# A graph network's layer pair: edge counts moved beside the keys, one addition moved forward, and one PSUM bank passed from the preparation to the groups' sums

## The chip, the cores and the metric

The kernel runs on one core of a Trainium2 chip. A core has TensorE (PE, matrix multiply; its weight loads are listed apart as PEld), VectorE (DVE), ScalarE (ACT), GpSimd (POOL) and queues for DMA, of which this kernel uses mainly SyncE's (SP). They run side by side and wait for one another by semaphores. SBUF is the memory that they work in; PSUM, eight banks of 128 x 512 float32, is where TensorE puts its results. The metric is device time in microseconds (us) of one execution.

## The reference

32 graphs ("batches") of 512 nodes with 128 features each, and a weight for each pair of nodes; about one weight in 16 is not zero. Cut to what matters:

```
# layer 0, for each batch
adj  = adj + I ; degree = adj.sum(2) ; dinv = degree ** -0.5
x    = layernorm(x + dinv * (adj @ (dinv * (x @ W0))) + b0)
# layer 1, for each batch, each pair of nodes i, j
pre  = (x_j @ W1[:128]) + (x_i @ W1[128:]) + b1          # 512 x 512 x 128
msg  = gelu(layernorm(pre) * g1 + be1)
agg  = sum over j of msg[i, j] * adj[i, j]
x    = layernorm(x + layernorm([x, agg] @ W2 + b2) * g2 + be2)
```

The degree of a node and the number of its edges (weights that are not zero) are both row sums, of the weights and of a mask. All of x, W and adj are float32.

## The kernel before, in words

**Groups.** The kernel works on edges only. The weights that aren't zero are sorted into "slots": in each block of 128 x 128 node pairs every row gives its t-th edge to slot t. A batch has 8 such slots of 4 groups, one slot of a single group (the node's own edge) and two slots of 4 groups for edges left over and gathered across rows: 41 groups a batch, called position 0 to 40 here, 1312 in all. A group takes four steps, each on its own engine, and one a turn later than the one before:

- `pairs` (lines 711 to 726, TensorE): 16 bf16 matmuls (lines 724 and 725) into one PSUM bank of the pool `ps_u`; from position 33 on 8 more instructions on float32 (line 720).
- `sums` (line 734, VectorE) adds a row of `ac` to that bank and writes `u_sb` in SBUF. That frees the bank. Positions 33 to 40 have no such step: there ScalarE reads the bank itself.
- `weights` (line 749, GpSimd) makes `sw`, `messages` (line 763, ScalarE) makes `m`, four activations.
- `aggregate` (line 772, TensorE) adds `m` times `sw` to the batch's sum `agg`, 8 instructions.

In the turn of group g the program issues pairs of g, aggregate of g-3, sums and weights of g-1, messages of g-2 (`pass_on`, lines 843 to 853).

**Preparation.** In the same turns other generators run in small steps (a step ends at each `yield`), and each has a stretch of turns in `plan` (lines 799 to 806): `layer0` of the next batch takes 26 steps in positions 0 to 21, `shared` of this batch 45 steps in positions 8 to 27, `lists`, `parts`, `factors` and `more` lie around the change of batch, and `finish` of the batch before goes step by step from position 2 on. Layer 0 transposes the weights (lines 249 and 261), sums the degrees (line 260), makes a mask of zeros (line 263), counts the edges by summing the mask (line 293, four ScalarE instructions for four blocks of rows), works out `dinv` on GpSimd (lines 277 to 287), adds x and b0 (line 289, GpSimd), scales (lines 297 and 302), multiplies (line 311), normalizes (lines 318 and 191 to 211) and makes the `key` by which edges are sorted (lines 357 to 366, four blocks of rows, one a step; lines 361 and 362 are VectorE's). The counts of edges are read by one line, 499 in `shared`, where they are compared with the edges listed.

**PSUM.** Eight banks: three for `pairs` (`ps_u`, line 80), one for `agg`, four for every result of the preparation (`ps`, line 82, through `bank`, line 213).

**Order.** Line 860 fixes the order of ScalarE, GpSimd and VectorE as the program issues it. The order of TensorE and of SyncE's queue is not written: a planner sets it when the program is built, by the program's order and by what it holds ready at a moment. The turns before the first group (line 838) lie outside line 860, and there the planner orders every engine.

## Time and profile before

| what | us |
|---|---|
| three runs: median (lowest, highest) | 4014.03 (4009.70, 4014.95) |
| the profiled execution, time | 4011.64 |
| its span on the core | 4009.9 |
| TensorE matmul busy in the span | 3766.3 (94%) |
| VectorE / ScalarE / GpSimd busy | 3263.9 / 2791.9 / 2225.5 |
| first matmul of the first group, from the span's start | 62.5 |

The profile is that of one execution. Busy time is the time in which an engine worked; a matmul's end is modelled, so that the share says little on how near TensorE is to its peak. A line of the waits names the engine and line that waited, what ended the wait, the total in us, how many times, and the longest one. A line of the timeline gives the start and the duration in us, engine, line, operation, tiles, shape and count, and in brackets the idle time before it with what ended it. Batch 16 serves as the example: its position 0 starts at 2023.3 us, its position 9 at 2046.7 and its position 14 at 2063.4.

### The profile page before, as it was taken

What the parts mean: (1) busy time and instruction counts of PE and PEld (TensorE: products, weight loads), DVE (VectorE), ACT (ScalarE), POOL (GpSimd) and SP (SyncE); (2) the same over time, 40 slices, a digit from 0 to 9 for tenths busy, and PEclk for the clock granted to TensorE, in tenths of its full rate; (3) what the DMA queues carried; (4) which work ended last, traced back from release to release, by engine and by line L of the source; (5) the groups of instructions that cost most, each with busy time, mean ns of one, the idle gap of its engine ahead of it and who ended that gap; (6) DMA issues with size and microseconds to landing.
All of it is one profiled execution on the core that took longest, in us unless ns stands there. A gap on an engine that the chain in (4) does not pass through costs nothing. (4 is left out here: it accounts for less than half of the span.)

```text
span 4009.9 us, 108439 instructions
## 1 busy us (share of the span) xinstructions
PE 3766.3 (94%) x39744; PEld 3510.3 (88%) x39744; DVE 3263.9 (81%) x10645; ACT 2791.9 (70%) x8321; POOL 2225.5 (55%) x2526
## 2 busy tenths in 40 slices
PE   5999999999999999999999999999999999999997
PEld 5988889888899888898888998888998889888887
DVE  6888888888887888888888888888888888788892
ACT  4777677676776766776767767667767677676664
POOL 4555565555655555655556555556555565555554
PEclk7999999999999999999999999999999999999998
DMA  3444444444444444444444444444444444444442
GB/s 85 107 109 106 114 101 106 107 107 105 113 102 106 108 106 110 106 106 106 107 105 113 102 106 108 106 112 104 106 105 108 105 108 106 108 107 105 98 105 56
DMA packets 902107, 419.99 MB, mean 105 GB/s; under 512 B 724304, under 2 KB 882192, under 8 KB 901568
## 3 DMA queue, kind: packets, MB, share of 16 engines
q1 hardware_dynamic: 901344, 412.52, 44.1%
q8 instruction: 317, 5.19, 0.5%
q14 instruction: 222, 1.82, 0.1%
q0 software_dynamic: 224, 0.46, 0.1%
HBM read 227.15 MB, written 13.76 MB: 60 GB/s over the span
## 5 line engine op out<-in xcount | busy, mean ns | idle before, releaser
L749 POOL TENSOR_TENSOR sw<-mt,a_t 128x512 f32<-128x512 bf16 x1056 | 1216.8, 1164 | 918.1 <-PE agg L772 764.0
L772 PE MATMUL agg<-sw,m 128*128 128x128 f32 x10496 | 1495.7, 285 | 76.2 <-POOL sw L749 46.1
L724 PE MATMUL u<-c,s 128*128 128x128 bf16 x15744 | 1433.9, 220 | 84.0 <-DVE u_sb L734 80.3
L763 ACT ACTIVATE m<-u_sb,r 128x128 f32<-128x128 f32 x4096 | 1294.0, 395 | 142.3 <-DVE u_sb L734 57.8
L772 PEld LDWEIGHTS agg<-sw,m 128*128 128x128 f32 x10496 | 1304.5, 192 | 94.2 <-POOL sw L749 51.3
L724 PEld LDWEIGHTS <-s 128*128 128x128 bf16 x15744 | 1191.2, 98 | 115.0 <-issue 40.9
L725 PE MATMUL u<-be,sd_rows 128*128 128x128 bf16 x5248 | 1148.6, 220 | 20.7 <-DMA sd_rows<-sd_ds 14.6
L734 DVE TENSOR_TENSOR u_sb<-u,ac 128x512 f32<-128x512 f32 x1056 | 713.4, 676 | 200.6 <-PE u L725 177.1
L725 PEld LDWEIGHTS <-sd_rows 128*128 128x128 bf16 x5248 | 512.7, 98 | 30.7 <-issue 20.0
L763 ACT ACTIVATE m<-u,r_s 128x128 f32<-128x128 f32 x1024 | 288.3, 363 | 251.6 <-PE agg L772 247.4
L533 ACT COPY sent<-pl 128x352 f32<-128x352 f32 x512 | 228.9, 447 | 315.9 <-PE pl L537 278.8
L687 DVE TENSOR_SCALAR s<-raw,node_p 128x2052 bf16<-128x2052 bf16 (+1 forms) x352 | 421.5, 1197 | 20.6 <-DMA raw<-idx_ds 11.9
L720 PE MATMUL u<-ac,sj 128*128 128x128 f32 x2048 | 437.8, 296 | 0.0
L749 POOL TENSOR_TENSOR sw<-mt,sent 128x512 f32<-128x512 bf16 x256 | 296.4, 1163 | 229.0 <-PE agg L772 176.2
L537 PEld LDWEIGHTS pl<-a_t,sj 128*128 128x128 f32 x2048 | 316.2, 191 | 60.7 <-issue 59.2
L457 DVE MAX8 a_t<-key 128x8 f32<-128x128 f32 x1024 | 301.2, 294 | 34.5
L537 PE MATMUL pl<-a_t,sj 128*128 128x176 f32 x2048 | 327.4, 313 | 1.3 <-POOL a_t L505 1.3
L522 DVE TENSOR_SCALAR sj<-pj,node_p 128x512 f32<-128x512 f32 x256 | 187.7, 745 | 153.8 <-PE pj L526 153.8
L720 PEld LDWEIGHTS u<-ac,sj 128*128 128x128 f32 x2048 | 310.0, 192 | 0.4
L458 DVE FIND_INDEX8 idx_m<-a_t,key 128x8 uint32<-128x128 f32 x1024 | 291.4, 285 | 0.0
L311 PEld LDWEIGHTS pconv<-s,a_t 128*128 128x128 f32 x1024 | 141.3, 214 | 57.1 <-ACT s L297 55.4
L361 DVE SCALAR_TENSOR_TENSOR key<-pv,a_sum,c_sum 128x512 f32<-128x512 f32 x128 | 95.7, 748 | 108.3 <-PE pv L365 108.3
(178 smaller groups left out, 4788.8 us busy)
## 6 DMA issues: line engine op xcount, KB each, us to landing
raw<-idx_d SPq DMA_DIRECT2D x256, 513.0 KB
raw<-idx_ds SPq DMA_DIRECT2D x64, 513.0 KB
a_nat<-in_adj_dram SPq DMA_DIRECT2D x32, 1024.0 KB
sd_rows<-sd_d SPq DMA_DIRECT2D x768, 12.0 KB
xs<-in_x_dram SPq DMA_DIRECT2D x32, 256.0 KB
out_dram<-o_sb SPq DMA_DIRECT2D x32, 256.0 KB
mt<-s SPq DMA_TRANSPOSE x352
raw<-idx_ds SPq DMA_DIRECT2D x32, 129.0 KB
```

The source lines that it names most:

```text
L457: nc.vector.max(found, k)
L458: nc.vector.max_index(idx[:, n, h : h + 8], found, k)
L533: nc.scalar.copy(sent[:, n - 1], pt[:, : SHARED * WIDE].rearrange("p (k w) -> p k w", w=WIDE))
L537: nc.tensor.matmul(pt[:, k * WIDE : (k + 1) * WIDE], sj[:, n, k * P : (k + 1) * P], at[:, n, :], start=True, stop=True,)
L687: nc.vector.tensor_scalar(s.rearrange("p (k e) -> p k e", k=3), raw, node_p, None, ALU.is_equal)
L720: nc.tensor.matmul(pu[:, c, :], place, state[b]["ac"][:, q, 0, :], start=first, stop=False)
L724: nc.tensor.matmul(pu[:, c, :], here, c3[:, k, c, :], start=(first and k == 0), stop=False)
L725: nc.tensor.matmul(pu[:, c, :], dev[:, q, c, :], be9, start=False, stop=(c == C - 1))
L734: nc.vector.tensor_tensor(u, pu, a if t == EXTRA else bcast(a[:, q, :], C), ALU.add)
L749: nc.gpsimd.tensor_tensor(sw, mt[:, 0] if t == EXTRA else mt[:, :, q, :], a, ALU.mult)
L763: nc.scalar.activation(m[:, c, :], u[:, c, :], AF.Gelu, scale=r[:, k : k + 1])
L772: nc.tensor.matmul(st["agg"][:, c, :], m[:, c, :], sw[:, c, :], start=(begin and c == 0), stop=(end and c == C - 1),)
```

## The change

Three edits. The four counts of edges leave the step of layer 0 that makes the scaled features (turn of position 6) and go one by one into the four steps that make the keys (positions 18 to 21), each in front of its two VectorE instructions; they read the same mask and write the same `edges`. The addition of x and b0 on GpSimd moves one step forward, ahead of the six small instructions on the degrees; the number of steps stays. `ps_u` gets four banks instead of three, and `ps` three instead of four. No instruction is added or taken away.

```diff
-    ps_u = ctx.enter_context(tc.tile_pool(name="ps_u", bufs=3, space=PSUM))
+    ps_u = ctx.enter_context(tc.tile_pool(name="ps_u", bufs=4, space=PSUM))
     ps_g = ctx.enter_context(tc.tile_pool(name="ps_g", bufs=1, space=PSUM))
-    ps = ctx.enter_context(tc.tile_pool(name="ps", bufs=4, space=PSUM))
+    ps = ctx.enter_context(tc.tile_pool(name="ps", bufs=3, space=PSUM))
...
-        yield from pause(2)
+        yield
+        xb = node.tile([P, C, D], F32, tag="t2", name=f"xb_{b}")
+        nc.gpsimd.tensor_tensor(xb, xs, bcast(rows["b0"], C), ALU.add)
+        yield
 
         deg1 = small.tile([P, C], F32, tag="deg1", name=f"deg1_{b}")
...
         nc.gpsimd.tensor_tensor(dinv2, dinv, dinv, ALU.mult)
-        xb = node.tile([P, C, D], F32, tag="t2", name=f"xb_{b}")
-        nc.gpsimd.tensor_tensor(xb, xs, bcast(rows["b0"], C), ALU.add)
-
-        for q in range(C):
-            copied = small.tile([P, N], BF16, tag="copied", name=f"counted_{b}_{q}", bufs=1)
-            nc.scalar.activation(copied, mask[:, q, :], AF.Copy, accum_out=edges[:, q : q + 1])
 
         s = node.tile([P, C, D], F32, tag="t1", name=f"s_{b}")
...
         for q in range(C + 1):
             if q:
+
+                copied = small.tile([P, N], BF16, tag="copied", name=f"counted_{b}_{q}", bufs=1)
+                nc.scalar.activation(copied, mask[:, q - 1, :], AF.Copy, accum_out=edges[:, q - 1 : q])
                 here = key[:, q - 1, :]
                 nc.vector.scalar_tensor_tensor(here, pt, a_sum[:, q - 1 : q], c_sum, ALU.add, ALU.add)
```

## The prediction

> **What bounds the kernel now.** I read the page's busy times first, then the waits, then the timeline of one batch, engine by engine.

> ```profile
> PE 3766.3 (94%) x39744; PEld 3510.3 (88%) x39744; DVE 3263.9 (81%) x10645; ACT 2791.9 (70%) x8321; POOL 2225.5 (55%) x2526
> ...
> PE u L724 <- DVE u_sb L734: 80.3, 69, 2.2
> PE agg L772 <- POOL sw L749: 46.1, 30, 1.6
> PE agg L772 <- ACT m L763: 30.0, 20, 1.5
> ```

> TensorE is the busiest, and its longest waits are those the bank edit aims at: pairs waiting until VectorE has emptied a bank of `ps_u`, 69 waits, two a batch. The next two answer them: aggregate waiting for GpSimd and ScalarE. The question is whether taking the first away saves time or lengthens the others. TensorE in batch 16, then VectorE, then GpSimd:

> ```profile
> 2044.19 0.33 PE L724 MATMUL u<-c,s 128*128 128x128 bf16 x3 [0.84 <-DVE u_sb L734]
> ...
> 2046.74 0.22 PE L724 MATMUL u<-c,s 128*128 128x128 bf16 x1 [1.50 <-DVE u_sb L734]
> ...
> 2065.97 1.16 PE L772 MATMUL agg<-sw,m 128*128 128x128 f32 x8 [1.55 <-POOL sw L749]
> ```

> ```profile
> 2032.42 0.69 DVE L641 TENSOR_TENSOR u<-pu,b_row 128x512 f32<-128x512 f32 x1 [2.05 <-PE pu L638]
> ...
> 2057.07 0.36 DVE L196 BATCH_NORM_AGGREGATE mv_l<-stats_l 128x2 f32<-128x6 f32 x4
> ```

> ```profile
> 2057.53 0.23 POOL L199 TENSOR_SCALAR ve_l<-mv_l 128x4 f32<-128x4 f32 x1 [3.39 <-DVE mv_l L196]
> ...
> 2064.75 2.29 POOL L749 TENSOR_TENSOR sw<-mt,a_t 128x512 f32<-128x512 bf16 x2
> ```

> ```profile
> 2032.40:2057.40 25.00, 22.66 (x250) 22.11 (x248) 24.30 (x91) 21.76 (x70) 17.85 (x21) 0.93 0.39 76
> 2057.40:2066.00 8.60, 7.05 (x89) 6.63 (x86) 8.57 (x26) 6.13 (x19) 7.64 (x16) 1.00 0.43 112
> 2066.00:2098.00 32.00, 31.99 (x270) 27.28 (x271) 18.09 (x27) 19.66 (x56) 11.34 (x10) 1.00 0.49 134
> ```

> Columns of the stretches: length, then busy us of PE, PEld, DVE, ACT, POOL. A chain shows. At 2032.42 VectorE gets the finish of the last batch from TensorE. From there it works 24.30 of 25.00 us without one wait, until the statistics of the next batch's layer 0. GpSimd, which had stood 3.39 us in front of them, works 7.64 of 8.60 us until the `sw` of group 11, and TensorE stands before that group's aggregate. From 2066 on TensorE never stops (31.99 of 32.00). Timed in batches 2 to 29 of the trace the pieces repeat: 22.87 (L641 to line 318) + 2.15 (to the last L196) + 0.40 + 8.07 (power of L187 to the end of `sw` 11) + 0.05 = 33.5 us, then 89.1 us of TensorE until the next L641, of which 88.6 is the least. So the waits at positions 8 and 9 lie inside a stretch that VectorE and GpSimd time: TensorE has 3.9 us to spare there (25.00 - 22.66, and 8.60 - 7.05), whatever it is spent on.

> [...]

> **The change part by part.** *Four banks for the sums.* Pairs 8 needs the bank of group 4 instead of 5, and 0.84 + 1.50 = 2.34 us a batch of waits go. TensorE then stands earlier at aggregate 10, which can't begin before `m` of group 10 (2061.07, behind the normalization on ScalarE), and at aggregate 11, whose `sw` ends at 2065.92 as before: nothing on VectorE or GpSimd in that chain moves. In an unchanged order the gain is nil. It is real only so far as work from behind aggregate 11 comes in front of it, and TensorE's order is the planner's. In the trace it keeps the program's order, except where something was late in its eyes (pairs 9 lies among the matmuls of line 311 and aggregate 5). With 2.3 us more in hand it will see aggregate 10 late, and it now has a bank to fill the gap: pairs 15 needs the sums of group 11 (2059.32 to 2060.00) instead of group 12 (2063.14 to 2063.82). It runs in the 1.5 us before aggregate 10, or in the gap before 11. One pairs is 16 matmuls, 0.055 us apart: 0.88 us. 31 batches have a next layer 0: 31 x 0.88 = 27.3 us. Ends: 0 (order kept) and 1.76 us a batch (pairs 16 too, its bank free at 2063.82), 54.6.

> *Counts on ScalarE.* Four times 0.75 us (starts 2043.20, 2043.93, 2044.69, 2045.44) leave the front of the scaled features. Those then wait for `dinv`, and `m` of group 5 comes 1.7 to 3 us sooner than 2048.07; aggregate 5 and line 311 follow. VectorE reads line 311's result at 2055.25 straight behind its own work, so this shortens nothing; it keeps TensorE from finding a new wait at aggregate 5. At the new place each count falls into ScalarE's waits for the shared lists (1.93 us, three a batch); the last has none, and delays the last copy of line 533 from 2097.72 to 2098.47, and VectorE's line 553, which needs that copy and now the count too (its output takes the mask's place), started at 2098.53. With the time of a semaphore I put 0.1 us a batch, as VectorE then works without a pause up to a short wait of TensorE at position 31: 3.1 us; ends 0 and 0.75 (23 us). Queued behind the last count are messages 20 and 21, whose aggregates come over 1.8 us after their old end.

> *x + b0.* 1.27 us of GpSimd move from behind the degrees to before `sw` 5, and `dinv` of batch 16's turn comes 1.27 us later, 2044.3: still before the old start of the scaling (2046.07). `sw` 5 has 9 us until its aggregate. Nothing, in the loop; without that cover it would cost 1.27 a batch.

> *Before the first group* both do help: the chain is serial there.

> ```profile
> 14.01 1.37 POOL L289 TENSOR_TENSOR xb<-xs,b_row 128x512 f32<-128x512 f32 x1
> ...
> 18.43 0.20 POOL L287 TENSOR_TENSOR dinv<-dinv 128x4 f32<-128x4 f32 x1
> ...
> 18.91 0.63 ACT L293 ACTIVATE counted<-mask 128x512 bf16<-128x512 bf16 x1
> 19.45 0.19 ACT L293 ACTIVATION_READ_ACCUMULATOR counted<-mask 128x1 f32 x1
> 19.54 1.12 ACT L297 ACTIVATE s<-psup,dinv 128x128 f32<-128x128 f32 x4
> ```

> `dinv` is there at 18.35 and the scaling starts at 19.54: 1.2 us, once (ends 0 and 2).

> *Three banks for the preparation.* I followed the banks through batch 16. Most are held at positions 14 to 20: a held chunk of the shared lists, a block of the keys, the chunk at work. At position 19 the third chunk (2088.69) finds the key's bank just free (2088.44), or else waits for the copy of the first (2088.73). The first transposes of layer 0 can't go ahead of the finish any more, but pairs 3 can fill that gap. I put 0; ends 0 and 0.65 us (one chunk without a second bank: copy 0.45 and 0.2 of waits) in each of four steps.

> Sum against the profiled 4011.6: - 27.3 + 3.1 - 1.2 = 3986.2. The median of the runs is 2.4 above the profiled one, so 3987 to 3989; I say 3987.

> **Rivals.** *The wait only moves*: TensorE's order stays, the 2.34 us reappear at aggregates 10 and 11. For it: the order departs from the program's in few places. 4014 + 3.1 - 1.2 = 4016. *Two groups come forward*: pairs 16 fits before aggregate 11 too, if the planner believes GpSimd as late as it is. 4014 - 54.6 + 2 = 3961. *Slower, the preparation starves*: at positions 18 to 21 a count of 0.75 us stands before the copy that holds a bank, beside the key's bank. If one chunk a step waits 0.4 us (between 0.05 and 0.65) in the stretch where TensorE has no slack: 4 x 0.4 x 31 = 50 us, 4014 - 26 + 50 = 4038. It decides from 0.22 us a step, where it eats the 0.88. Against it: the times above leave room of 0.15 us or more. The change does do what it says; only its worth hangs on the order.

> **How the numbers follow.** Forecast 0.50, two groups 0.15, moved wait 0.15, starved 0.20. Runs tell a change of about 0.2% (8 us) from none: faster 0.65, same 0.15, slower 0.20. The range runs from 3955, under the two groups' time, to 4026, which holds the moved wait and the mild part of the starved case; some 0.05 below and 0.13 above are left. The forecast's own range is 3975 to 4000.

> **What would show it.** Right: no pairs waiting for L734 at positions 8 and 9; on TensorE pairs 15 before aggregate 11; the wait of L772 for `sw` still there and GpSimd's 8.07 us unchanged; from aggregate 11 to the next L641 88.2 instead of 89.1; the first pairs at 61.3 instead of 62.5. Wrong: pairs 15 behind aggregate 11 (moved wait), TensorE waiting at L537, L526 or L365 for a copy or for L361 (starved), or a chain from L641 to `sw` 11 that isn't 33.5 any more.

## The result, and the profile after

The changed kernel takes 4019.82 us (median; 4016.50 to 4021.18), the kernel before on the same chip 4012.14 (4008.56 to 4018.11). The ratio is 1.0017, 95% interval 1.0009 to 1.0024: slower by 7 us, where 25 less was forecast. The span of the profiled execution is 4017.3 us, 7.4 more than before.

The page of the changed kernel, busy times (us, share of the span, instructions):

```profile
PE 3792.3 (94%) x39744; PEld 3525.4 (88%) x39744; DVE 3265.4 (81%) x10645; ACT 2783.8 (69%) x8321; POOL 2226.0 (55%) x2526
```

TensorE is busy 26.0 us longer with the same 39744 matmuls. Its waits in the changed kernel:

```profile
PE agg L772 <- ACT m L763: 68.0, 35, 2.1
PE agg L772 <- POOL un L645: 43.2, 30, 1.4
...
PE agg L772 <- POOL sw L749: 6.3, 7, 1.5
...
PE u L724 <- DVE u_sb L734: 3.0, 3, 2.0
```

What the fourth bank was to remove is gone: 80.3 us of pairs waiting for line 734 have become 3.0. In its place aggregates wait: 68.0 us for messages (30.0 before), and 43.2 in a new place, aggregate 5 in position 8. (GpSimd's line 645 is named because it happens to end then; ScalarE starts message 5 only at 2054.26, behind the scaled features, and the aggregate goes at 2054.86.) So the wait moved. TensorE also waits 31 times now for the scaled features at line 308 (20.7 us in all). TensorE in batch 16 of the changed kernel:

```profile
2069.50 1.48 PE L772 MATMUL agg<-sw,m 128*128 128x128 f32 x8 [2.11 <-ACT m L763]
...
2072.05 0.53 PE L724 MATMUL u<-c,s 128*128 128x128 bf16 x3
...
2073.86 1.16 PE L772 MATMUL agg<-sw,m 128*128 128x128 f32 x8
...
2075.28 0.33 PE L724 MATMUL u<-c,s 128*128 128x128 bf16 x3
```

The first line is aggregate 10, the third aggregate 11. Pairs 14 (from 2072.05) and pairs 15 (from 2075.28) lie behind them as before. The bank that pairs 15 needs was free from 2067.90 on, when the sums of group 11 ended on VectorE; it was not used. After the wait of 2.11 us, three matmuls take 0.53 us that take 0.33 later on: in the trace they start 0.107 us apart instead of 0.056. The stretches of this batch, cut as in the prediction (length, busy us of PE, PEld, DVE, ACT, POOL, then TensorE's granted clock):

```profile
2040.30:2065.30 25.00, 23.09 (x277) 22.65 (x275) 24.29 (x91) 19.00 (x62) 17.87 (x21) 1.00 0.37 85
2065.30:2073.90 8.60, 6.49 (x59) 5.83 (x56) 8.56 (x26) 6.14 (x19) 7.65 (x16) 0.80 0.35 89
2073.90:2105.90 32.00, 31.99 (x269) 27.09 (x269) 18.00 (x26) 21.26 (x60) 11.34 (x10) 1.00 0.55 133
```

VectorE works 24.29 of 25.00 (24.30 before), then GpSimd 7.65 of 8.60 (7.64): the chain in front of aggregate 11 is the old one. Over batches 2 to 29 its pieces are 22.86 + 2.15 + 0.40 + 8.07 + 0.05 us against 22.87 + 2.15 + 0.40 + 8.07 + 0.05. New in the second stretch is a granted clock of 0.80. Pairs 14 runs slowly and fills the gap in front of aggregate 11, so the waits for `sw` fall from 46.1 to 6.3 us although `sw` comes no sooner. Over the whole execution the mean granted clock is 0.979 instead of 0.985; 0.006 x 4017 us is 24 us, by my estimate most of the 26.0 us that TensorE is busy longer.

Where the 7.4 us of span came from, from the starts in both traces: aggregate 11 to the next line 641 takes 89.38 us on the mean of 31 batches instead of 89.07 (31 x 0.304 = +9.4). Line 641 to aggregate 11 gives back 0.03 a batch (-0.9). The first pairs start at 66.2 instead of 62.5 (+3.7), and the first and last batch are 1.6 and 3.2 us shorter. Their sum is +7.4.

### The profile page after: what moved, and what is told of

Same layout as the page of the kernel before. It is cut to its first block, busy times and chain, and to the rows that moved or that the text cites. A ratio compares the mean times of both kernels' runs of the same rounds, so it can differ in the third digit from the quotient of the medians.

```text
span 4017.3 us, 108437 instructions
## 1 busy us (share of the span) xinstructions
PE 3792.3 (94%) x39744; PEld 3525.4 (88%) x39744; DVE 3265.4 (81%) x10645; ACT 2783.8 (69%) x8321; POOL 2226.0 (55%) x2526
## 5 line engine op out<-in xcount | busy, mean ns | idle before, releaser
L749 POOL TENSOR_TENSOR sw<-mt,a_t 128x512 f32<-128x512 bf16 x1056 | 1217.0, 1164 | 921.7 <-PE agg L772 813.7
L772 PE MATMUL agg<-sw,m 128*128 128x128 f32 x10496 | 1500.8, 285 | 118.0 <-ACT m L763 68.0
L763 ACT ACTIVATE m<-u_sb,r 128x128 f32<-128x128 f32 x4096 | 1293.4, 394 | 213.2 <-DVE counts L484 105.1
L724 PE MATMUL u<-c,s 128*128 128x128 bf16 x15744 | 1431.7, 221 | 7.6 <-DVE s L687 4.4
L772 PEld LDWEIGHTS agg<-sw,m 128*128 128x128 f32 x10496 | 1304.6, 193 | 145.9 <-POOL ve_l L199 67.8
L724 PEld LDWEIGHTS <-s 128*128 128x128 bf16 x15744 | 1203.1, 99 | 103.3 <-issue 38.8
L734 DVE TENSOR_TENSOR u_sb<-u,ac 128x512 f32<-128x512 f32 x1056 | 713.6, 676 | 198.5 <-PE u L725 180.2
L763 ACT ACTIVATE m<-u,r_s 128x128 f32<-128x128 f32 x1024 | 288.4, 363 | 249.6 <-PE agg L772 246.2
L749 POOL TENSOR_TENSOR sw<-mt,sent 128x512 f32<-128x512 bf16 x256 | 296.4, 1163 | 233.6 <-PE agg L772 188.8
L537 PEld LDWEIGHTS pl<-a_t,sj 128*128 128x128 f32 x2048 | 316.1, 190 | 66.5 <-issue 37.0
L537 PE MATMUL pl<-a_t,sj 128*128 128x176 f32 x2048 | 333.9, 315 | 0.4 <-POOL a_t L505 0.4
L361 DVE SCALAR_TENSOR_TENSOR key<-pv,a_sum,c_sum 128x512 f32<-128x512 f32 x128 | 95.7, 748 | 111.9 <-PE pv L365 111.9
L308 PE MATMUL pconv<-s,a_t 128*128 128x128 f32 x1024 | 141.8, 283 | 20.7 <-ACT s L294 20.7
```

Source lines behind the costliest of these rows:

```text
L537: nc.tensor.matmul(pt[:, k * WIDE : (k + 1) * WIDE], sj[:, n, k * P : (k + 1) * P], at[:, n, :], start=True, stop=True,)
L724: nc.tensor.matmul(pu[:, c, :], here, c3[:, k, c, :], start=(first and k == 0), stop=False)
L734: nc.vector.tensor_tensor(u, pu, a if t == EXTRA else bcast(a[:, q, :], C), ALU.add)
L749: nc.gpsimd.tensor_tensor(sw, mt[:, 0] if t == EXTRA else mt[:, :, q, :], a, ALU.mult)
L763: nc.scalar.activation(m[:, c, :], u[:, c, :], AF.Gelu, scale=r[:, k : k + 1])
L772: nc.tensor.matmul(st["agg"][:, c, :], m[:, c, :], sw[:, c, :], start=(begin and c == 0), stop=(end and c == C - 1),)
```

## The experiments

Twelve kernels ran, in three sets of four, each set with the kernel before on the same chip (4011.3, 4013.5 and 4013.6 us); a ratio is to that. I held two theories first. A: the chain on VectorE and GpSimd sets the stretch, the fourth bank is worth nothing unless TensorE's order changes, and the bank taken from the preparation costs 0.2 us a batch. B: the banks do gain, and the moves of the counts or the lost bank take more back.

**Banks alone.** The kernel before with

```diff
-    ps_u = ctx.enter_context(tc.tile_pool(name="ps_u", bufs=3, space=PSUM))
+    ps_u = ctx.enter_context(tc.tile_pool(name="ps_u", bufs=4, space=PSUM))
...
-    ps = ctx.enter_context(tc.tile_pool(name="ps", bufs=4, space=PSUM))
+    ps = ctx.enter_context(tc.tile_pool(name="ps", bufs=3, space=PSUM))
```

> Only the banks are changed (four for the sums, three for the preparation); counts and x + b0 stay where they were. Theory A (the chain on VectorE and GpSimd sets the stretch in front of aggregate 11, so the fourth bank is worth nothing, and the third bank of the preparation costs about 0.2 us a batch at lines 537 and 526): 4012 + 31 x 0.2 = 4018, no pairs waiting for line 734, 33.5 us from line 641 to aggregate 11 as before, and 89.3 us from there to the next line 641. Theory B (the banks do gain and the counts in the key's steps take it back): faster than before, 4005 or less. First pairs at 62.5 if the later start of the changed kernel comes from the moves, at 66 if from TensorE's clock by chance or from the banks.

4019.45 us, ratio 1.0019 (1.0011 to 1.0028): all of the slowdown. Aggregate 11 to line 641 takes 89.35 us. One part of theory A's expectation failed. The waits for line 734 are not gone:

```profile
PE u L724 <- DVE u_sb L734: 49.0, 36, 2.0
```

They have moved from pairs 8 and 9 to pairs 10 (1.5 us a batch). It takes the fourth bank and the moves together to remove them, and the time is the same with and without them.

**Moves alone.** The changed kernel with `ps_u` 3 and `ps` 4.

> Only the two moves (counts beside the keys, x + b0 ahead of the degrees); three banks for the sums and four for the preparation as before. Theory A: the moves cost nothing in the loop; 4012 with the first pairs at 62.5, or 4016 with the first pairs at 66 if the moves are what delays the start. Theory B (the counts cost the gain of the banks): over 4018, with 0.2 us a batch or more between aggregate 11 and the next line 641.

4011.15 us, ratio 1.0001 (0.9993 to 1.0010): the counts beside the keys and the earlier x + b0 cost nothing and gain nothing. Aggregate 11 to line 641: 89.01 us.

**Seven banks.** The changed kernel with three and three.

```diff
-    ps_u = ctx.enter_context(tc.tile_pool(name="ps_u", bufs=4, space=PSUM))
+    ps_u = ctx.enter_context(tc.tile_pool(name="ps_u", bufs=3, space=PSUM))
```

> The changed kernel with the fourth bank of the sums taken away again and not given to anyone: three and three. Theory A: the fourth bank is worth nothing, so this takes what the changed kernel takes, 4020 within 3, with the waits for line 734 back (about 2.3 us a batch) and those of the aggregates shorter by as much. Theory B (the fourth bank gains, and the third bank of the preparation loses more): slower than the changed kernel, up to 31 x 2.3 = 71 us if the whole wait counts, 4047 if one pairs a batch does.

4018.84 us, ratio 1.0021 (1.0014 to 1.0027), no more than the changed kernel. The waits of this kernel:

```profile
PE agg L772 <- ACT m L763: 64.9, 31, 2.1
PE u L724 <- DVE u_sb L734: 51.8, 39, 2.2
PE agg L772 <- POOL sw L749: 30.6, 20, 1.5
```

51.8 us of waiting for a bank are back and cost nothing: with and without them the kernel takes the same time. The fourth bank was worth nothing here, and theory B falls. Where the third bank of the preparation is missed shows between aggregates 14 and 15 of batch 16. The kernel before, stretch and timeline:

```profile
2076.70:2080.59 3.89, 3.89 (x37) 3.36 (x35) 3.86 (x6) 1.29 (x5) 1.16 (x1) 1.00 0.80 282
```

```profile
2078.51 1.36 PE L537 MATMUL pl<-a_t,sj 128*128 128x176 f32 x8
```

and the changed kernel:

```profile
2084.58:2088.68 4.10, 4.10 (x37) 3.36 (x35) 4.07 (x7) 1.50 (x5) 1.17 (x1) 1.00 0.76 229
```

```profile
2086.38 1.57 PE L537 MATMUL pl<-a_t,sj 128*128 128x176 f32 x8
```

The same 37 matmuls take 0.21 us longer, inside the eight of line 537: the fifth of them starts at 2087.09, and the trace gives as its releaser line 522 on VectorE, which reads out a bank of `ps` until 2087.03. In the kernel before it has no releaser. This repeats in each batch (means 3.89 and 4.10; 4.10 in all three kernels with three banks for the preparation, 3.89 with moves alone). 31 x 0.21 = 6.5 us of the 7.7 between the medians. Aggregates 11 to 14 and 15 to 22 are the same within 0.01 us, apart from 0.04 behind aggregate 11.

**Pairs 15 ahead, by hand, in both kernels.** So far A says what the banks don't do. Whether the prediction's mechanism was right, had the order come, needs the order:

```diff
+    ahead = {}
...
-                pu = pairs(b, t, q, made_s[b, t], made_d[b, t])
+                pu = ahead.pop(n, None)
+                if pu is None:
+                    pu = pairs(b, t, q, made_s[b, t], made_d[b, t])
+                if n == 14:
+                    for k in range(n + 1, n + 2):
+                        t_k, q_k = order[k]
+                        ahead[k] = pairs(b, t_k, q_k, made_s[b, t_k], made_d[b, t_k])
                 pass_on()
```

In the changed kernel:

> The changed kernel with the pairs of position 15 issued ahead of aggregate 11, by hand, in each batch: the order that my prediction expected of the planner. Theory A (the mechanism of the prediction is right, only the order wasn't taken): 16 matmuls of 0.055 us move into the hole in front of aggregate 11 in 31 batches, 4020 - 27 = 3993, and aggregate 11 to the next line 641 takes 88.5 instead of 89.4. Theory C (no hole is left that such work can use, or aggregate 11 is pushed back by as much): 4020 or more, with the piece from line 641 to aggregate 11 longer than 33.8.

4003.14 us, ratio 0.9979 (0.9969 to 0.9988) to the kernel before. Against the changed kernel that is 0.38% or 15 us, about half of what A expected, and C (no hole that such work can use) is not it either. Aggregate 11 to line 641 fell to 88.32, by 1.06 us, but the piece ahead rose from 33.77 to 34.36. TensorE in this kernel, timeline and stretches of 1 us:

```profile
2062.64 1.27 PE L772 MATMUL agg<-sw,m 128*128 128x128 f32 x8 [2.11 <-ACT m L763]
...
2064.95 0.53 PE L724 MATMUL u<-c,s 128*128 128x128 bf16 x3
...
2066.65 0.53 PE L724 MATMUL u<-c,s 128*128 128x128 bf16 x3
...
2067.84 1.11 PE L772 MATMUL agg<-sw,m 128*128 128x128 f32 x8
```

```profile
2065.00:2066.00 1.00, 1.00 (x11) 1.00 (x10) 1.00 (x5) 1.00 (x4) 0.92 (x3) 0.50 0.49 100
```

Aggregate 11 now starts straight behind pairs 15, without a wait: pairs 14 (from 2064.95) and the first matmuls of pairs 15 (from 2066.65) ran at a granted clock of 0.50 (third column from the end), until 2067.24, and filled more than the hole. That became theory E: what limits the changed kernel beside A is the low clock behind the wait of 2.11 us. The kernel before, whose longest waits there are 1.5 us, has no such drop at aggregate 10 in batches 1 to 30. The changed kernel has it in 27 of them.

The trace of this run already has the comparison that tells. In 25 of batches 1 to 30 TensorE waits 2.1 us in front of aggregate 10. In 22 of these the low clock follows, and aggregate 11 comes 34.34 us behind line 641. In the other three it doesn't follow: aggregate 11 comes at 33.53, and 0.65 us of the hole are left. Kernel, order and wait are the same; the clock alone differs. The next set was made to test A and E by edits.

The same edit in the kernel before, three banks:

> The kernel before, three banks for the sums, with the pairs of position 15 issued ahead of aggregate 11 by hand. In the trace of before the bank that they need is read out at 2063.82 and aggregate 11 starts at 2065.97, with TensorE at full clock (16 matmuls of pairs in 0.88 us). Theory A (the order is what pays, the fourth bank isn't needed for it): 31 x 0.88 = 27 us faster than before, 3984, more than what the same order brought in the changed kernel, where TensorE came out of a wait of 2.11 us at a lower clock. Theory B (the fourth bank is what lets pairs 15 forward): no gain, 4011 or more, with waits for line 734 in front of pairs 15.

3983.55 us, ratio 0.9926 (0.9912 to 0.9939): 30 us, the 27 in full and a little more, and without a fourth bank.

```profile
2047.07 1.27 PE L772 MATMUL agg<-sw,m 128*128 128x128 f32 x8 [1.52 <-ACT m L763]
...
2049.72 0.33 PE L724 MATMUL u<-c,s 128*128 128x128 bf16 x3
...
2051.42 1.16 PE L772 MATMUL agg<-sw,m 128*128 128x128 f32 x8 [0.65 <-POOL sw L749]
```

In this timeline pairs 15 (from 2049.72) runs at full clock ahead of aggregate 11, and 0.65 us of the 1.55 us hole are left. No pairs 15 waits for a bank. Aggregate 11 to line 641 takes 88.11 us, 0.96 less than in the kernel before, and the piece in front of it does not grow (33.77, 33.80 in the kernel before).

**Pairs 14 ahead too, changed kernel.** If the wait of 2.11 us, which the low clock followed in 27 of 30 batches, is cut short, E expects the full gain. Pairs 14 goes ahead of aggregate 10, pairs 15 ahead of aggregate 11. The diff is against the changed kernel.

```diff
+    ahead, EARLY = {}, {13: (14,), 14: (15,)}
...
-                pu = pairs(b, t, q, made_s[b, t], made_d[b, t])
+                pu = ahead.pop(n, None)
+                if pu is None:
+                    pu = pairs(b, t, q, made_s[b, t], made_d[b, t])
+                for k in EARLY.get(n, ()):
+                    t_k, q_k = order[k]
+                    ahead[k] = pairs(b, t_k, q_k, made_s[b, t_k], made_d[b, t_k])
                 pass_on()
```

> The changed kernel with pairs 14 issued ahead of aggregate 10 as well as pairs 15 ahead of aggregate 11. The wait in front of aggregate 10 is then filled with 0.88 us of pairs, 2.11 becomes 1.2. Theory E (what halved the gain of the run with pairs 15 alone was the lower clock behind the wait of 2.11 us): the clock stays up, aggregate 11 isn't pushed back (33.8 us behind line 641, not 34.4), and the gain against the changed kernel is 31 x 1.06 = 33 us, 3987. If it was something else: 4003, as with pairs 15 alone.

3989.65 us, ratio 0.9939 (0.9926 to 0.9953), 31 us less than the changed kernel. No drop at aggregate 10 in any of batches 1 to 30. TensorE in this kernel:

```profile
2053.92 1.27 PE L772 MATMUL agg<-sw,m 128*128 128x128 f32 x8 [1.22 <-ACT m L763]
...
2055.69 0.33 PE L724 MATMUL u<-c,s 128*128 128x128 bf16 x3
...
2058.30 1.16 PE L772 MATMUL agg<-sw,m 128*128 128x128 f32 x8 [1.56 <-POOL sw L749]
```

The wait is 1.22, pairs behind it run at 0.33 for three, and aggregate 11 stands 33.81 us behind line 641. That is what E expects. By itself this run would not be proof, because it also takes pairs 14 out of the slow place, which leaves less to do in front of aggregate 11. Together with the batches of the run before (34.34 against 33.53 us), E holds: the low clock took about half of the gain.

**The GpSimd half of the chain.** Theory A says that aggregate 11 moves with `sw` 11. First try: all `sw` one turn earlier.

```diff
-            summed.append((key, sums(*key, pu), weights(*key)))
+            summed.append((key, sums(*key, pu), made_w.pop(key)))
...
                 pass_on()
+                made_w[b, t, q] = weights(b, t, q)
                 gathered_c.append(((b, t, q), pu))
```

> The changed kernel with each group's weights on GpSimd (sw) issued one turn earlier, so that sw 11 no longer stands behind the two small ops of the shared lists in GpSimd's queue. Message 11 is there at 2072.5 in the trace of the changed kernel, aggregate 11 starts at 2073.86. Theory A (the chain of the prediction alone, aggregate 11 then goes with its message): 1.3 us a batch, 4020 - 40 = 3980. Theory E (TensorE, slowed after its wait of 2.11 us, ends pairs 14 only at 2073.66 and is the next bound): 0.2 us a batch, 4013.

> The kernel before with the same edit: sw one turn earlier. Here TensorE ends pairs 14 at 2064.4 at full clock and message 11 is there at about 2064.7, against 2065.97 for aggregate 11. Theory A and theory E agree: 1.3 us a batch, 4011 - 39 = 3972. If the chain on GpSimd isn't what sets the stretch: 4011.

Both missed: 4035.42 us (ratio 1.0057, 1.0043 to 1.0070) and 4021.44 (1.0017, 1.0011 to 1.0024). `sw` 11 did come early: power of line 187 to its end is 2.77 us instead of 8.07 in the second kernel. But the edit put one more `sw` ahead of line 649 in GpSimd's queue, too. VectorE in the second kernel:

```profile
2063.37 0.87 DVE L194 BATCH_NORM_STATS2 stats_l<-un 128x6 f32<-128x128 f32 x4 [1.14 <-POOL un L649]
2064.16 0.36 DVE L196 BATCH_NORM_AGGREGATE mv_l<-stats_l 128x2 f32<-128x6 f32 x4
2064.44 1.09 DVE L318 SCALAR_TENSOR_TENSOR y<-pconv,dinv,xb 128x128 f32<-128x128 f32 x4
```

VectorE stands 1.14 us for GpSimd, which it hardly did before (one such wait in the kernel before, 31 here), and line 318 comes 23.66 us behind line 641 instead of 22.87. The edit broke one link and lengthened the next. The low clock came as well: in 18 of batches 1 to 30 of the second kernel it follows a wait of 2.4 us in front of aggregate 10, and aggregate 11 stands 34.10 us behind line 641; in the other 12 it stands at 33.14, against 33.55 in the kernel before. So where the clock stayed up the edit did bring aggregate 11 forward. As a whole it tests A badly, so it was done again with less.

**Three small GpSimd ops later.** Lines 499 to 501 (0.75 us in the queue ahead of `sw` 11, wanted by nobody soon) go behind the loop over `ended`.

```diff
-        nc.gpsimd.tensor_tensor(missed, missed, st["edges"], ALU.add)
-        nc.gpsimd.tensor_scalar(missed, missed, -1000.0, None, ALU.mult)
-        nc.gpsimd.tensor_tensor(most[:, C * C :], most[:, C * C :], missed, ALU.add)
...
+        nc.gpsimd.tensor_tensor(missed, missed, st["edges"], ALU.add)
+        nc.gpsimd.tensor_scalar(missed, missed, -1000.0, None, ALU.mult)
+        nc.gpsimd.tensor_tensor(most[:, C * C :], most[:, C * C :], missed, ALU.add)
         sj_f = sj.rearrange("p n e -> p (n e)")
```

> The kernel before with the same edit on GpSimd. TensorE stands at full clock here and ends pairs 14 1.55 us ahead of aggregate 11, message 11 is there 1.2 us ahead. Theory A and theory E: 31 x 0.75 = 23 us less, 3989. If the lower clock sets in here too once aggregate 11 isn't waited for: 4005.

3989.84 us, ratio 0.9939 (0.9926 to 0.9953), as expected. The power to `sw` 11 takes 7.33 instead of 8.07, and line 641 to aggregate 11 is 0.73 shorter. So GpSimd's queue is in the chain, op by op. In the changed kernel:

> The changed kernel with the three ops of GpSimd that add up the missed edges (lines 499 to 501, 0.75 us between the power of the second normalization and sw 11) issued after the loop over the ends of the lists instead of before it, so that sw 11 comes 0.75 us earlier; nothing else on GpSimd moves ahead. Theory A (GpSimd's chain alone sets aggregate 11): 31 x 0.75 = 23 us less, 3997. Theory E (TensorE at its lower clock behind the wait of 2.11 us ends pairs 14 at 2073.66 and has only 0.2 us left to aggregate 11): 31 x 0.2 = 6 us less, 4014.

4006.49 us, ratio 0.9981 (0.9972 to 0.9989): 14 us less than the changed kernel, between the two. The low clock came in 18 of batches 1 to 30 at aggregate 10. In those aggregate 11 stands 33.31 us behind line 641, in the other 12 it stands at 32.80, against 33.53 in the changed kernel: 0.22 and 0.73 us gained, what E and what A expect of a batch. E named the limit, but took it for every batch.

**Both on the kernel before.**

> The kernel before with pairs 15 ahead of aggregate 11 and the same edit on GpSimd. With pairs 15 in place 0.65 us of waiting for sw 11 are left, and sw 11 comes 0.75 us sooner: 31 x 0.65 = 20 us less than with pairs 15 alone, 3963, with message 11 or pairs 15 as the last in front of aggregate 11. If another wait follows at once: 3980 or more.

3962.42 us, ratio 0.9875 (0.9860 to 0.9890), the best of all and 21 us less than pairs 15 ahead alone, where 20 were expected. GpSimd, then TensorE in it:

```profile
2036.56 1.04 POOL L187 TENSOR_TENSOR rstd_l<-ve_l,power 128x4 f32<-128x4 f32 x1
...
2039.55 2.30 POOL L749 TENSOR_TENSOR sw<-mt,a_t 128x512 f32<-128x512 bf16 x2
```

```profile
2040.77 1.16 PE L772 MATMUL agg<-sw,m 128*128 128x128 f32 x8
```

`sw` 11 follows after two ops (starting 2039.55), and aggregate 11 goes with no wait.

**The place of the banks.** With four banks for the sums the first pairs had come at 65.3 to 66.3 us in all five profiles so far, with three at 62.5 to 63.3 in four of five. This kernel moves the pools and no instruction.

```diff
+    ps = ctx.enter_context(tc.tile_pool(name="ps", bufs=3, space=PSUM))
     ps_u = ctx.enter_context(tc.tile_pool(name="ps_u", bufs=4, space=PSUM))
     ps_g = ctx.enter_context(tc.tile_pool(name="ps_g", bufs=1, space=PSUM))
-    ps = ctx.enter_context(tc.tile_pool(name="ps", bufs=3, space=PSUM))
```

> The changed kernel with the pool of the preparation's three banks declared ahead of the sums' four: the same instructions in the same order on every engine, only the places of the banks differ. If the place of the preparation's banks is what lowers TensorE's clock between 20 and 40 us in kernels with four banks for the sums (first pairs at 65.3 to 66.3 instead of 62.5 to 63.3): first pairs at 63, 4016. If not: first pairs at 66, 4020.

4018.80 us, ratio 1.0013 (1.0007 to 1.0020), first pairs at 66.0: the place of the banks is not it. The stretch from 20 to 25 us in the changed kernel, and in the kernel before:

```profile
20.00:25.00 5.00, 5.00 (x23) 5.00 (x24) 0.00 (x0) 1.72 (x7) 1.27 (x1) 0.50 0.83 261
```

```profile
20.00:25.00 5.00, 5.00 (x32) 4.97 (x32) 0.00 (x0) 1.69 (x7) 1.27 (x1) 0.71 0.83 260
```

At a clock of 0.50 TensorE gets 23 matmuls through, at 0.71 32. In the trace the clock is low from 15.6 to 25.8 us in the changed kernel and from 16.0 to 22.9 in the kernel before: 10.24 us against 6.83. All 14 profiles agree: up to 45 us the clock is low for 13.7 us in the five kernels that start early, and for 17.1 to 23.9 us in the nine that start late. Two kernels with three banks (`sw` early and missed edges later, on the kernel before) also started at 66.3 and 65.8. So the later start needs no fourth bank. Why it was there in all seven profiles with four banks, and in two of seven with three, stays open.

## Why the prediction was wrong

**The step that failed** is in "Four banks for the sums": that the planner, with 2.3 us and a bank in hand, would see aggregate 10 late and put pairs 15 in the gap, 27.3 us. It kept pairs 14 and 15 behind aggregates 10 and 11, and the gain is the 0 that stood as the lower end. What the planner weighed wasn't tried; a trace doesn't tell it. The rival "the wait only moves", to which I gave 0.15, is what happened. That its 4016 comes near is in part luck: it has 3.1 us for the counts, which cost nothing, and lacks the 6.5 that the lost bank took.

**What the step rested on held.** The chain of 33.5 us is there to two hundredths (33.53, 33.55 in the kernel before), and pairs 15 is worth its 0.88 us a batch and a little more, 0.96, where it was put ahead by hand: 3983.55 us. But the bank was not what it lacked. The prediction itself has the sums of group 12, whose bank pairs 15 needs with three banks, ending at 2063.82, and that is 2.15 us ahead of aggregate 11 (2065.97). With three banks the order was open, too, and I did not draw the conclusion.

**Three banks for the preparation**: put at 0 with ends of 0 and 0.65 us in each of four steps. It is 0.21 us a batch, in the first of those steps alone (line 537, between pairs 17 and 18, where I had looked at position 19), 6.5 us in all: the bank that line 522 reads out last is not free in time there. This term alone makes the result slower instead of the same.

**Counts**: 3.1 us, ends 0 and 23. The moves alone show 0 (interval -3 to +4 us). That message 5 would keep TensorE from a new wait at aggregate 5 did not hold: message 5 comes 1.7 us sooner behind line 641, TensorE comes sooner still and waits 43.2 us there in all. Inside the stretch that the chain sets, that costs nothing. **x + b0**: nothing, right. **Before the first group**: -1.2 us, and it is 0. There the planner orders ScalarE as well, and it left the counts ahead of the scaling, in the changed kernel at

```profile
19.48 0.19 ACT L359 ACTIVATION_READ_ACCUMULATOR counted<-mask 128x1 f32 x1
19.57 1.12 ACT L294 ACTIVATE s<-psup,dinv 128x128 f32<-128x128 f32 x4
```

against 19.54 before. Twice I counted on the planner to use a freedom, and twice it kept its order.

**The sum as it came out**: 4012.1 + 31 x 0.21 = 4018.6, with about 1 us left of the measured 4019.8. The range held the time because it reached as far as the moved wait and a mildly starved preparation; the sign was wrong, at 0.65 for faster.

**Missed altogether**: that where the waits go matters to TensorE's clock. In batch 16 two waits of 0.84 and 1.50 us, at pairs 8 and 9, became one of 1.44 at aggregate 5 and one of 2.11 at aggregate 10, and the 16 matmuls of pairs 14 behind it took almost twice as long (0.107 us apart instead of 0.056). In the changed kernel this stays hidden behind the chain: aggregate 11 stands 33.53 us behind line 641 in the 27 batches with the low clock and 33.52 in the three without it. With pairs 15 put ahead in that kernel it took about half of what the order brings.

## What to carry to other kernels

In this kernel a bank and an earlier operand only opened an order; where another program decides the order, the step to predict is that program's, and its current order is a good first guess (it was kept twice here). Ask of each freed wait which operand ends last behind it, and what moves with that. Before a buffer is taken from elsewhere, test the wanted order by hand with the buffers as they are: here two reorderings with the old banks gave 1.25%, giving the bank away cost 0.19%.

## What the runs showed of the hardware

In the traces of the kernel before and of the changed kernel TensorE's granted clock is 1.00 or 0.50 and nothing between. Of their 52 low stretches 40 last 3.41 us and ten are 2 to 8 times as long; the end of the execution cuts the other two. Waits of 2.10 to 2.13 us in front of aggregate 10 were followed by a low stretch in 27 of 30 batches of the changed kernel, and waits of 2.1 us there in 13 of 30 with moves alone and in 10 of 30 with seven banks. The 19 waits of 1.51 to 1.54 us there in the kernel before were followed by none. So the length of a wait of 2.1 us did not decide alone.
